# Layer 0 of a graph network: whole-array and half-array products in alternation, one-hots in batches

## The chip, the cores and the metric

The kernel runs on one core of a Trainium2 chip. The metric is device time in microseconds (us) of a whole execution; the median of three runs is compared. Engines are named as the profile names them: PE does matrix products (PEld is its weight load), DVE is the vector engine, ACT the scalar engine, POOL the GpSimd engine, SP the one that issues most DMAs.

## The reference

A graph has 12,500 nodes with 64 features and 212,500 directed edges sorted by destination. Three layers each add up the features of a node's sources, divide by their count and mix with two small matrices; after them, the edges' own attributes are averaged per node and a three-layer perceptron follows.

```python
def _sage_conv(x, src, dst, Wl, Wr, b, n_nodes):
    msgs = x[src]
    summed = jax.ops.segment_sum(msgs, dst, num_segments=n_nodes)
    cnt = jax.ops.segment_sum(jnp.ones(src.shape[0], x.dtype), dst, num_segments=n_nodes)
    agg = summed / jnp.maximum(cnt, 1.0)[:, None]
    return agg @ Wl + x @ Wr + b

h = jnp.maximum(_layernorm(x, axis=-1), 0.0)
x = x + _L0_gnn_ref(h, edge_index, Wl, Wr, b)     # three _sage_conv, relu between
h = jnp.maximum(_layernorm(x, axis=-1), 0.0)
x = x + _L1_gnn_ref(h, edge_index, edge_attr_64, W0, b0, W1, b1, W2, b2)
```

## The kernel before

Nodes are cut into 98 blocks of 128 (`NB`). The sums over edges are done as dense products: the adjacency is written out as a matrix of small counts in 8 bits, two of them in one 16-bit word, and every sum is a product of node rows with a column stripe of that matrix. Layer 0 builds the matrix, uses each stripe from on-chip memory as soon as it is complete, and stores it to DRAM; layers 1 and 2 load the stripes again.

**A stage of layer 0** is one pair of destination blocks (`hp`, 49 of them, a stripe of 256 columns). The rows are held as three bf16 parts of 64 columns each, so that their sum carries the full number. `dense` therefore makes two products per source block: the first two parts together, 128 weight columns, over the whole array into `p1` (L234), and the third part, 64 columns, over half of the array into one half of `p2` (L243). The half alternates with the source block's number, so two neighbouring half products can run at the same time. In the kernel before, all 98 whole products come first, then ACT copies `p1` to `e1` (L239), then come all 98 half products, and DVE adds both into `agg` (L248).

**Building the next stripe** is woven into the stage's 196 products. A list of "fills" has a due time each, as a fraction of the stage; `woven` calls a fill when the products emitted so far reach it. Twenty-six of them are `pair`s: DVE makes for each of two groups of edges a one-hot `c` of 245 columns (L439) and a one-hot with weight `h` of 128 columns (L443), PE multiplies them into `pb` (L447), and ACT writes the counts into the stripe `m` (L450). The 27th stores the stripe through SP's queue. The one-hots have six buffers each, `pb` three, `m` three.

**The other fills.** `turn` (due at 0.05) transposes the stage before's own rows with a half-array product (L260), and `finish` (0.15) mixes `agg` and these rows with the layer's weights (`mix`, L269 and L273, both whole-array) and cuts the result into the three parts for layer 1. `index(j)` (due at 0.6 of every second stage) finds the edges of four destination blocks: one comparison over all tile heads on DVE (L340), three gathers on POOL (L330), counts on DVE, five small products (L397) and a transpose (L406) on PE, and the unpacking of the transposed code into `lo`, `weight` and `col` on DVE (L408 to L426). Its result is used two stages later.

PE's order is the order in which the program is written (`manual_schedule`); a planner orders the other engines' queues. Ahead of the first stage the first two `index` calls, a layer norm over all rows (14 groups, mostly on DVE) and the first stripe are done.

**Layers 1 and 2** call the same `dense` with four destination blocks (512 columns) and loaded stripes.

Of the kernel before, what the change touches and what calls it, by code (L numbers as in the profile page):

```python
# [9 lines left out]
F32 = mybir.dt.float32  # L10
I32 = mybir.dt.int32
BF16 = mybir.dt.bfloat16
# [3 lines left out]
ALU = mybir.AluOpType  # L16
AX = mybir.AxisListType
PSUM = bass.MemoryType.PSUM
# [3 lines left out]
P = 128  # L22
D = 64
# [11 lines left out]
QW, Q5 = 26, 24  # L35
WD = 5
# [24 lines left out]
def in_order(  # L61
# [24 lines left out]
    nc = tc.nc  # L86
    NB, T, EP = sz.nb, sz.t, sz.ep
    NL = Wl.shape[0]
    assert NB % 2 == 0
    HP = NB // 2  # L90
    CW = HP * WD
    NG = -(-NB // 4)
# [104 lines left out]
    ps_d = ctx.enter_context(tc.tile_pool(name="ps_dense", bufs=1, space=PSUM))  # L197
    ps_c = ctx.enter_context(tc.tile_pool(name="ps_conv", bufs=1, space=PSUM))
# [30 lines left out]
    def dense(rows, at, n):  # L229


        p1 = ps_d.tile([P, 4 * P], F32, name="p1")[:, :n]
        for i in range(NB):
            nc.tensor.matmul(  # L234
                p1, rows[:, i, : 2 * D], at(i), start=i == 0, stop=i == NB - 1
            )
            yield
        e1 = conv_p.tile([P, 4 * P], F32, name="e1", bufs=1)[:, :n]
        nc.scalar.copy(e1, p1)  # L239
        p2 = ps_d.tile([P, 4 * P], F32, name="p2")[:, :n]  # L240
        for i in range(NB):
            half = slice(D * (i % 2), D * (i % 2) + D)
            nc.tensor.matmul(  # L243
                p2[half], rows[:, i, 2 * D :], at(i), start=i < 2, stop=i >= NB - 2
            )
            yield
        agg = conv_p.tile([P, 4 * P], F32, name="agg")[:, :n]
        nc.vector.tensor_tensor(agg, e1, p2, op=ALU.add)  # L248
        return agg

    def conv(layer, rows, agg, j0, n):

        ht = hts[conv.turn]
        conv.turn ^= 1

        def turn():
            pt = ps_c.tile([D, 4, P], F32, name="pt")
            for k in range(n):
                for i in range(3):
                    nc.tensor.matmul(  # L260
                        pt[:, k, :], rows[:, j0 + k, D * i : D * i + D], identb,
                        start=i == 0, stop=i == 2,
                    )
            nc.scalar.copy(ht[:D, :n, :], pt[:, :n, :])

        def mix():
            po = ps_c.tile([P, 2, 4, D], F32, name="po")
            for k in range(n):
                nc.tensor.matmul(  # L269
                    po[:, 0, k, :], agg[:, k * P : (k + 1) * P], wl2[:, layer, :],  # L270
                    start=True, stop=True,
                )
                nc.tensor.matmul(  # L273
                    po[:, 1, k, :], ht[:, k, :], wr1[:, layer, :], start=True, stop=True
                )
            o = conv_p.tile([P, 4, D], F32, name="o")[:, :n, :]
            nc.vector.tensor_tensor(  # L277
                o, po[:, 0, :n, :], inv[:, j0 : j0 + n, None].to_broadcast([P, n, D]), op=ALU.mult
            )
            nc.vector.tensor_tensor(o, o, po[:, 1, :n, :], op=ALU.add)  # L280
            return o

        return turn, mix
# [19 lines left out]
    with ExitStack() as s:  # L303
        idx = s.enter_context(tc.tile_pool(name="idx", bufs=2))
        ps_b = s.enter_context(tc.tile_pool(name="ps_build", bufs=3, space=PSUM))
        ps_i = s.enter_context(tc.tile_pool(name="ps_idx", bufs=1, space=PSUM))
        hot = s.enter_context(tc.tile_pool(name="hot", bufs=6))
        ln = s.enter_context(tc.tile_pool(name="ln", bufs=1))
# [16 lines left out]
        mats = s.enter_context(tc.tile_pool(name="mats", bufs=3))  # L325
# [9 lines left out]
        def index(j):  # L335
# [53 lines left out]

# [4 lines left out]
            )  # L394
            pi = ps_i.tile([P, 2, P], F32, name="pi")
# [15 lines left out]
            lo = idx.tile([P, P], F32, name="lo")  # L411
            weight = idx.tile([P, P], F32, name="weight")
            col = idx.tile([P, P], F32, name="col")
            nc.vector.tensor_scalar(a, ci, P - 1, None, op0=ALU.bitwise_and)
            nc.vector.tensor_copy(lo, a)
# [3 lines left out]
            nc.vector.tensor_scalar(weight, b, 255.0, 1.0, op0=ALU.mult, op1=ALU.add)  # L419
# [6 lines left out]
            nc.vector.scalar_tensor_tensor(col, a, float(WD), b, op0=ALU.mult, op1=ALU.add)  # L426
            return lo, weight, col

        def build(m, block, codes):

            lo, weight, col = codes
            off = P * (block % 2)

            def pair(q):
                pb = ps_b.tile([P, 2, 256], F32, name="pb")
                for i in range(2):
                    w = 32 * (block % 4) + q + i
                    c = hot.tile([P, CW], BF16, name="c")
                    nc.vector.tensor_scalar(  # L439
                        c, iota_c, col[:, w : w + 1], None, op0=ALU.is_equal  # L440
                    )
                    h = hot.tile([P, P], BF16, name="h")
                    nc.vector.tensor_scalar(  # L443
                        h, iota_l, lo[:, w : w + 1], weight[:, w : w + 1],
                        op0=ALU.is_equal, op1=ALU.mult,
                    )
                    nc.tensor.matmul(pb[:, i, :CW], h, c, start=True, stop=True)  # L447
                k = WD if q < Q5 else WD - 1
                o = off + WD * q - max(q - Q5, 0)
                nc.scalar.copy(  # L450
                    m[:, :, o : o + 2 * k].rearrange("p h (w d) -> p h w d", d=k),
                    pb[:, :, :CW].rearrange("p w (h d) -> p h w d", d=WD)[:, :, :, :k],
                )

            return [lambda q=q: pair(q) for q in range(0, QW, 2)]

        codes = {}
# [15 lines left out]
        def start_rows(a0):  # L473
            n = min(LG, NB - a0)
            xb = ln.tile([P, n, D], F32, name="xb", bufs=2)
            nc.sync.dma_start(xb, xv[:, a0 : a0 + n, :])
            relu_parts(ln, normed(ln, xb, n), parts[0][:, a0 : a0 + n, :])

        codes[0] = index(0)
        for a0 in range(0, NB, LG):  # L480
            start_rows(a0)
        with tc.manual_schedule(engines={PE}):
            codes[1] = index(1)
            m, fills = matrix(0)
            for f in fills:
                f()
            later = []
            for hp in range(HP):
# [4 lines left out]
                if hp % 2 == 0 and hp // 2 + 2 < NG:  # L493
                    j = hp // 2 + 2
                    fills.append((0.6, lambda j=j: codes.__setitem__(j, index(j))))
                view = m.bitcast(FP8)
                agg = woven(
                    dense(parts[0], lambda i: view[:, i // 2, i % 2 :: 2], 2 * P), fills
                )
                turn, mix = conv(0, parts[0], agg, 2 * hp, 2)  # L500
# [46 lines left out]
    with ExitStack() as s:  # L547
        mats = s.enter_context(tc.tile_pool(name="mats2", bufs=9, reuse_waits="tile"))
# [14 lines left out]
        with tc.manual_schedule(engines={PE}):  # L563
            later = []
            for g in range(NG):
                j0, n = 4 * g, min(4, NB - 4 * g)
                at = columns(g)
                agg = woven(dense(parts[1], at, n * P), later)
                turn, mix = conv(1, parts[1], agg, j0, n)
# [113 lines left out]
            for g in range(NG):  # L683
# [5 lines left out]
                agg = woven(dense(parts[0], at, n * P), fills)  # L689
                turn, mix = conv(2, parts[0], agg, j0, n)  # L690
# [569 lines left out]
```

## Time and profile before

| what | value |
|---|---|
| median of 3 runs | 3512.79 us (3512.18 to 3514.45) |
| the profiled execution | 3514.05 us, of which the span from first to last instruction is 3512.3 us |
| granted PE clock, mean over the span | 0.992 |
| PE busy / DVE busy / ACT busy / POOL busy | 3350.0 / 2111.3 / 1196.0 / 750.7 us |
| first product of layer 0, last L248 of layer 0 | 104.01 us, 1444.33 us |
| first product of layer 1 | 1450.66 us |

Times inside an execution count from its first instruction. A line such as "L243" is a line of the kernel before. In the timeline a row merges neighbouring instructions of one line: start, length, engine, line, operation, tiles, shape, count, and in brackets how long the engine had been idle and what ended that. An instruction's length on PE is modelled and longer than the distance to the next one, so distances between starts are what counts. In a group's row the part after the first bar is the total busy time and the mean length of one in nanoseconds, and after the second the idle time before them.

### The profile page before, as it was taken

What the parts mean: (1) busy time and instruction counts of PE and PEld (TensorE: products, weight loads), DVE (VectorE), ACT (ScalarE), POOL (GpSimd) and SP (SyncE); (2) the same over time, 40 slices, a digit from 0 to 9 for tenths busy, and PEclk for the clock granted to TensorE, in tenths of its full rate; (3) what the DMA queues carried; (4) which work ended last, traced back from release to release, by engine and by line L of the source; (5) the groups of instructions that cost most, each with busy time, mean ns of one, the idle gap of its engine ahead of it and who ended that gap; (6) DMA issues with size and microseconds to landing.
All of it is one profiled execution on the core that took longest, in us unless ns stands there. A gap on an engine that the chain in (4) does not pass through costs nothing.

```text
span 3512.3 us, 69396 instructions
## 1 busy us (share of the span) xinstructions
PE 3350.0 (95%) x26430; PEld 2019.0 (57%) x26430; DVE 2111.3 (60%) x9072; ACT 1196.0 (34%) x2101; POOL 750.7 (21%) x482
## 2 busy tenths in 40 slices
PE   1899999999999999999999999979999999999998
PEld 0566777777777777555454545544555555555555
DVE  8999999999999999300000000035556555555554
ACT  4555555555555555100000000022322322322232
POOL 1000000000000000000000000055555565555562
PEclk9999999999999999999999999989999999999999
DMA  2222222332223223645454545455455555555551
GB/s 45 115 116 118 115 116 115 137 129 115 115 120 146 115 111 134 233 155 220 155 212 165 202 176 191 170 218 181 176 182 211 204 206 181 176 183 211 204 193 53
DMA packets 168554, 555.12 MB, mean 158 GB/s; under 512 B 57793, under 2 KB 60386, under 8 KB 161938
## 3 DMA queue, kind: packets, MB, share of 16 engines
q1 hardware_dynamic: 133232, 478.53, 35.7%
q0 software_dynamic: 19648, 66.90, 5.6%
q10 hardware_dynamic: 15330, 5.16, 0.6%
q8 instruction: 208, 3.41, 0.4%
q14 instruction: 136, 1.11, 0.1%
HBM read 389.97 MB, written 160.56 MB: 157 GB/s over the span
## 4 chain that ended last, share of the span: by engine, by line
PE 84%; DVE 10%; issue 4%; DMA 1%; ACT 1%; POOL 0%; ACTq 0%; SPq 0%; DVEq 0%; POOLq 0%
PE p L234 40%; PE p L243 24%; PE pb L447 8%; PE pe L631 5%; DVE h L443 2%; DVE c L439 2%; PE po L273 2%; PE po L269 2%; PE pt L260 2%; DVE own L627 2%; PE ph L666 1%; PE mo L674 1%; DVE lower L340 0%; DVE junk L385 0%; PE mt L659 0%
## 5 line engine op out<-in xcount | busy, mean ns | idle before, releaser
L234 PEld LDWEIGHTS <-parts 128*128 128x128 bf16 x9702 | 937.2, 99 | 584.7 <-issue 46.2
L234 PE MATMUL p<-t,parts 128*128 128x512 fp8e3 (+1 forms) x4900 | 1106.7, 376 | 4.6 <-DMA t<-mat 4.6
L450 ACT CAST m<-pb 128x490 uint16<-128x490 f32 (+1 forms) x1274 | 717.4, 563 | 537.3 <-PE pb L447 534.4
L627 DVE TENSOR_SCALAR own<-iota_l,eplace 128x128 bf16<-128x128 bf16 x1862 | 548.2, 353 | 401.8 <-PE pe L631 401.4
L443 DVE TENSOR_SCALAR h<-iota_l,lo,weight 128x128 bf16<-128x128 bf16 x2548 | 779.8, 306 | 0.0
L439 DVE TENSOR_SCALAR c<-iota_c,col 128x245 bf16<-128x245 bf16 x2548 | 716.5, 281 | 10.9 <-PE pb L447 5.5
L243 PEld LDWEIGHTS <-parts 128*64 128x64 bf16 x9702 | 494.1, 109 | 387.8 <-issue 185.1
L234 PE MATMUL p<-m,parts 128*128 128x256 fp8e3 x4802 | 652.3, 273 | 0.6 <-ACT m L450 0.6
L243 PE MATMUL p<-t,parts 128*64 128x512 fp8e3 (+1 forms) x4900 | 584.4, 378 | 0.0
L447 PE MATMUL pb<-c,h 128*128 128x245 bf16 x2548 | 499.0, 274 | 52.4 <-DVE h L443 35.0
L248 DVE TENSOR_TENSOR agg<-e,p 128x256 f32<-128x256 f32 (+1 forms) x99 | 54.4, 549 | 603.2 <-PE p L243 600.3
L243 PE MATMUL p<-m,parts 128*64 128x256 fp8e3 x4802 | 409.3, 281 | 0.0
L602 POOL DMA_INDIRECT raw<-in_edge_dram,mine x98 | 93.7, 956 | 1124.9 <-DMA t<-mat 1098.6
L447 PEld LDWEIGHTS <-h 128*128 128x128 bf16 x2548 | 205.6, 98 | 204.0 <-DVE h L443 148.9
L613 POOL TENSOR_TENSOR erest<-raw,cut 128x1216 f32<-128x1216 f32 x98 | 244.2, 2492 | 202.2 <-issue 198.1
L631 PE MATMUL pe<-cut,own 128*128 128x192 bf16 x1862 | 227.0, 248 | 34.9 <-DVE own L627 17.5
L631 PEld LDWEIGHTS <-own 128*128 128x128 bf16 x1862 | 151.3, 98 | 166.4 <-issue 58.6
L615 POOL TENSOR_TENSOR cut<-erest,cut 128x1216 bf16<-128x1216 f32 x98 | 244.6, 2496 | 11.2 <-ACT cut L614 2.6
L612 ACT CAST cut<-raw 128x1216 bf16<-128x1216 f32 x98 | 118.1, 1205 | 275.6 <-PE pe L631 266.0
L277 DVE TENSOR_TENSOR o<-po,inv 128x128 f32<-128x128 f32 (+1 forms) x99 | 35.1, 354 | 271.8 <-PE po L273 271.6
L614 ACT CAST cut<-erest 128x1216 bf16<-128x1216 f32 x98 | 118.1, 1205 | 225.6 <-POOL erest L613 225.6
L330 POOL DMA_INDIRECT to<-in_dst_dram,at_i x25 | 23.6, 946 | 709.6 <-DVE at_i L358 595.8
(143 smaller groups left out, 1666.8 us busy)
## 6 DMA issues: line engine op xcount, KB each, us to landing
t<-mat SPq DMA_DIRECT2D x686, 448.0 KB, 6.1
mat<-m SPq DMA_DIRECT2D x49, 3136.0 KB, 10.0
xb<-in_x_dram SPq DMA_DIRECT2D x14, 224.0 KB, 2.7
xr<-in_x_dram ACTq DMA_DIRECT2D x24, 128.0 KB, 2.2
out_dram<-o SPq DMA_DIRECT2D x24, 128.0 KB, 2.0
raw<-in_edge_dram,mine POOLq DMA_INDIRECT x98, 5.4
eto<-in_dst_dram,mine POOLq DMA_INDIRECT x98, 3.7
here<-in_dst_dram ACTq DMA_DIRECT2D x4, 208.0 KB, 5.5
```

The lines of the kernel that those rows point to most:

```text
L234: nc.tensor.matmul(p1, rows[:, i, : 2 * D], at(i), start=i == 0, stop=i == NB - 1)
L243: nc.tensor.matmul(p2[half], rows[:, i, 2 * D :], at(i), start=i < 2, stop=i >= NB - 2)
L439: nc.vector.tensor_scalar(c, iota_c, col[:, w : w + 1], None, op0=ALU.is_equal)
L443: nc.vector.tensor_scalar(h, iota_l, lo[:, w : w + 1], weight[:, w : w + 1], op0=ALU.is_equal, op1=ALU.mult,)
L447: nc.tensor.matmul(pb[:, i, :CW], h, c, start=True, stop=True)
L450: nc.scalar.copy(m[:, :, o : o + 2 * k].rearrange("p h (w d) -> p h w d", d=k), pb[:, :, :CW].rearrange("p w (h d) -> p h w d", d=WD)[:, : ...
L612: nc.scalar.copy(cut[:, :, :D], raw)
L613: nc.gpsimd.tensor_tensor(rest, raw, cut[:, :, :D], op=ALU.subtract)
L614: nc.scalar.copy(cut[:, :, D : 2 * D], rest)
L615: nc.gpsimd.tensor_tensor(cut[:, :, 2 * D :], rest, cut[:, :, D : 2 * D], op=ALU.subtract)
L627: nc.vector.tensor_scalar(o, iota_l, place[:, k : k + 1], 1.0 / UNIT, op0=ALU.is_equal, op1=ALU.mult,)
L631: nc.tensor.matmul(state["p"], o, cut[:, k, :], start=k == 0, stop=k == EK - 1)
```

## The change

- `dense` takes a step. In layer 0 it is 2: two whole products, then the two half products of the same source blocks, and so on. In layers 1 and 2 the step is all blocks, which is the order before.
- `p1` and `p2` of layer 0 have two buffers. To make room[...], the turn and the mix share one tile and `pb` has two buffers.
- The one-hots of a block's 26 groups are made in three batches of 10, 8 and 8, each by three DVE operations on two tensors: `c`, `h`, and `h` times weight. `lo`, `weight` and `col` are kept in bf16, each number twice in a row, so that a batch can read them as pairs; `c` is one column wider (246). The batches have two buffers.
- `index` ends before its PE work; `by_edge` does that and the unpacking, one stage later.
- The layer norm's buffers are released before the stages start, and `m` has two buffers.

```diff
-    def dense(rows, at, n):
-        p1 = ps_d.tile([P, 4 * P], F32, name="p1")[:, :n]
-        for i in range(NB):
-            nc.tensor.matmul(
-                p1, rows[:, i, : 2 * D], at(i), start=i == 0, stop=i == NB - 1
-            )
-            yield
-        e1 = conv_p.tile([P, 4 * P], F32, name="e1", bufs=1)[:, :n]
-        nc.scalar.copy(e1, p1)
-        p2 = ps_d.tile([P, 4 * P], F32, name="p2")[:, :n]
-        for i in range(NB):
-            half = slice(D * (i % 2), D * (i % 2) + D)
-            nc.tensor.matmul(
-                p2[half], rows[:, i, 2 * D :], at(i), start=i < 2, stop=i >= NB - 2
-            )
-            yield
+    def dense(pool, rows, at, n, step):
+        p1 = pool.tile([P, n], F32, name="p1")
+        p2 = pool.tile([P, n], F32, name="p2")
+        for i0 in range(0, NB, step):
+            blocks = range(i0, min(i0 + step, NB))
+            for i in blocks:
+                nc.tensor.matmul(
+                    p1, rows[:, i, : 2 * D], at(i), start=i == 0, stop=i == NB - 1
+                )
+                yield
+            if i == NB - 1:
+                e1 = conv_p.tile([P, 4 * P], F32, name="e1", bufs=1)[:, :n]
+                nc.scalar.copy(e1, p1)
+            for i in blocks:
+                half = slice(D * (i % 2), D * (i % 2) + D)
+                nc.tensor.matmul(
+                    p2[half], rows[:, i, 2 * D :], at(i), start=i < 2, stop=i >= NB - 2
+                )
+                yield
...
-            pt = ps_c.tile([D, 4, P], F32, name="pt")
+            if layer:
+                pt = pool.tile([D, 4, P], F32, name="pt")
+                space["po"] = pool.tile([P, 2, 4, D], F32, name="po")
+            else:
+                both = pool.tile([P, 2, 2 * P], F32, name="pt_po")
+                pt = both[:D, 0, :].rearrange("p (k n) -> p k n", n=P)
+                space["po"] = both[:, 1, :].rearrange("p (i k d) -> p i k d", i=2, d=D)
...
-        ps_b = s.enter_context(tc.tile_pool(name="ps_build", bufs=3, space=PSUM))
+        ps_d = s.enter_context(tc.tile_pool(name="ps_dense", bufs=2, space=PSUM))
+        ps_c = s.enter_context(tc.tile_pool(name="ps_conv", bufs=1, space=PSUM))
+        ps_b = s.enter_context(tc.tile_pool(name="ps_build", bufs=2, space=PSUM))
         ps_i = s.enter_context(tc.tile_pool(name="ps_idx", bufs=1, space=PSUM))
-        hot = s.enter_context(tc.tile_pool(name="hot", bufs=6))
-        ln = s.enter_context(tc.tile_pool(name="ln", bufs=1))
+        hot = s.enter_context(tc.tile_pool(name="hot", bufs=2))
...
-            lo = idx.tile([P, P], F32, name="lo")
-            weight = idx.tile([P, P], F32, name="weight")
-            col = idx.tile([P, P], F32, name="col")
+            lo = idx.tile([P, P, 2], BF16, name="lo")
+            weight = idx.tile([P, P, 2], BF16, name="weight")
+            col = idx.tile([P, P, 2], BF16, name="col")
+            twice = lambda t: t[:, :, None].to_broadcast([P, P, 2])
...
+            cuts = [(0, 10), (10, 18), (18, QW)]
+            ready = {}
+
+            def hots(q0, q1):
+                n = q1 - q0
+                w = 32 * (block % 4) + q0
+                pairs = lambda t, k: t.rearrange("p (k t) -> p k t", t=2)[:, None].to_broadcast(
+                    [P, n, k // 2, 2]
+                )
+                own = lambda t, k: t[:, w : w + n, None, :].to_broadcast([P, n, k // 2, 2])
+                split = lambda t: t[:, :n].rearrange("p w (k t) -> p w k t", t=2)
+                c = hot.tile([P, 10, CW], BF16, name="c")
+                nc.vector.tensor_tensor(
+                    split(c), pairs(iota_c, CW), own(col, CW), op=ALU.is_equal
+                )
+                h = hot.tile([P, 10, P], BF16, name="h")
+                nc.vector.tensor_tensor(split(h), pairs(iota_l, P), own(lo, P), op=ALU.is_equal)
+                nc.vector.tensor_tensor(split(h), split(h), own(weight, P), op=ALU.mult)
+                for i in range(n):
+                    ready[q0 + i] = (h[:, i, :], c[:, i, : HP * WD])
 
             def pair(q):
+                for cut in cuts:
+                    if q == cut[0]:
+                        hots(*cut)
                 pb = ps_b.tile([P, 2, 256], F32, name="pb")
                 for i in range(2):
-                    w = 32 * (block % 4) + q + i
-                    c = hot.tile([P, CW], BF16, name="c")
-                    nc.vector.tensor_scalar(
-                        c, iota_c, col[:, w : w + 1], None, op0=ALU.is_equal
-                    )
-                    h = hot.tile([P, P], BF16, name="h")
-                    nc.vector.tensor_scalar(
-                        h, iota_l, lo[:, w : w + 1], weight[:, w : w + 1],
-                        op0=ALU.is_equal, op1=ALU.mult,
-                    )
-                    nc.tensor.matmul(pb[:, i, :CW], h, c, start=True, stop=True)
+                    h, c = ready[q + i]
+                    nc.tensor.matmul(pb[:, i, : HP * WD], h, c, start=True, stop=True)
...
-                if hp % 2 == 0 and hp // 2 + 2 < NG:
-                    j = hp // 2 + 2
-                    fills.append((0.6, lambda j=j: codes.__setitem__(j, index(j))))
+                j = hp // 2 + 2
+                if j < NG and hp % 2 == 0:
+                    fills.append((0.6, lambda j=j: found.__setitem__(j, index(j))))
+                elif j < NG:
+                    fills.append((0.6, lambda j=j: codes.__setitem__(j, by_edge(j, *found[j]))))
                 view = m.bitcast(FP8)
                 agg = woven(
-                    dense(parts[0], lambda i: view[:, i // 2, i % 2 :: 2], 2 * P), fills
+                    dense(ps_d, parts[0], lambda i: view[:, i // 2, i % 2 :: 2], 2 * P, 2), fills
                 )
...
-                agg = woven(dense(parts[1], at, n * P), later)
+                agg = woven(dense(ps_d, parts[1], at, n * P, NB), later)
```

## The prediction

> **What bounds the kernel now.** I read the 40 slices first. Layer 0 fills slices 2 to 16; there PE and DVE are both at 9, later PE alone is.
>
> ```profile
> PE   1899999999999999999999999979999999999998
> DVE  8999999999999999300000000035556555555554
> PEclk9999999999999999999999999989999999999999
> ```
>
> PE's busy time is modelled, so it cannot say which of the two sets layer 0. The waits between 104 and 1446 us can: PE waits for DVE 14.3 + 11.5 + 4.3 + 1.7 us and for ACT 0.6 us, 32 us in all. One stage (a pair of destination blocks, 49 of them) ends with L248: from 424.3 to 1213.8 us there are 30 of these, so a stage takes 789.5 / 29 = 27.2 us (27.4 over the whole layer, early stages being slower). **PE sets layer 0**, with DVE close behind.
>
> What PE spends a stage on, its timeline shows (start, length, instructions merged by line, count; L234 whole-array, L243 half-array, L447 one-hot products, L260 the turn, also half-array):
>
> ```profile
> 806.96 0.82 PE L234 MATMUL p<-m,parts 128*128 128x256 fp8e3 x6
> 807.71 0.52 PE L260 MATMUL pt<-identb,parts 128*64 128x128 bf16 x6
> 808.16 0.28 PE L234 MATMUL p<-m,parts 128*128 128x256 fp8e3 x1
> ...
> 819.40 0.93 PE L234 MATMUL p<-m,parts 128*128 128x256 fp8e3 x7
> 820.16 0.37 PE L447 MATMUL pb<-c,h 128*128 128x245 bf16 x2
> 820.37 0.93 PE L234 MATMUL p<-m,parts 128*128 128x256 fp8e3 x7
> 821.14 0.37 PE L447 MATMUL pb<-c,h 128*128 128x245 bf16 x2
> 821.44 0.63 PE L243 MATMUL p<-m,parts 128*64 128x256 fp8e3 x8
> 822.99 0.56 PE L447 MATMUL pb<-c,h 128*128 128x245 bf16 x2 [0.92 <-DVE c L439]
> 823.48 0.62 PE L243 MATMUL p<-m,parts 128*64 128x256 fp8e3 x7
> 824.03 0.38 PE L447 MATMUL pb<-c,h 128*128 128x245 bf16 x2
> 824.35 0.62 PE L243 MATMUL p<-m,parts 128*64 128x256 fp8e3 x7
> 824.90 0.38 PE L447 MATMUL pb<-c,h 128*128 128x245 bf16 x2
> ...
> 1438.68 5.54 PE L243 MATMUL p<-m,parts 128*64 128x256 fp8e3 x98
> 1444.05 0.50 PE L260 MATMUL pt<-identb,parts 128*64 128x128 bf16 x6
> ```
>
> Read starts, not lengths. Seven whole products take 820.16 - 819.40 = 0.76 us, 0.109 each; a pair of L447 among them takes 0.21. Half products run two at a time: 98 take 5.37 us, 0.109 per slot of two. Seven of them (four slots, 0.44) and a pair (0.21) should take 0.65 us, but the period is 824.90 - 824.03 = 0.87. **Leaving half-array mode and coming back costs 0.22 us.** The turn says the same without an L447: six whole products end by 807.61, L260 starts at 807.71; its six at 0.055 end by 808.04, L234 starts at 808.16. Single starts in the trace split it: 0.093 + 0.025 us going in, 0.096 + 0.010 coming out, **0.225 us a round trip**, the smaller terms being the first weight load that nothing hides. None of these instructions waits for another engine.
>
> [...] No row here shows a bf16 two-tensor operation; the change lays its scalars out as adjacent equal pairs[...].
>
> **The change part by part.**
>
> Turns by twos. In the instruction order of the old program layer 0 has 696 runs of half-array work, 14.2 a stage: one per gap between L447 pairs, and the turn. In the new order it has 2689, 54.9 a stage: one for every two blocks, the turn merged into one, and 5.9 where a fill falls between two half products. Outside the first stage that is 47 x 40.7 + 48 (the last stage has no fills) = 1961 more round trips: x 0.225 = **+441 us**, all on PE, which already sets the time. Splitting a slot of two costs 0.109; the new order has 288 splits, the old, by its odd runs, 192: **+10 us**. L447 pairs that now stand next to whole products are counted by this already. If the exposed first loads vanish in runs of two, a trip costs 0.19 and the first term is 373[...].
>
> One-hots batched. Gone: per stage 52 x (L439 + L443); starts 0.415 us apart in DVE's timeline, 21.6 us.
>
> ```profile
> L443 DVE TENSOR_SCALAR h<-iota_l,lo,weight 128x128 bf16<-128x128 bf16 x2548 | 779.8, 306 | 0.0
> L439 DVE TENSOR_SCALAR c<-iota_c,col 128x245 bf16<-128x245 bf16 x2548 | 716.5, 281 | 10.9 <-PE pb L447 5.5
> ```
>
> Added per block: three batches of 10, 8 and 8, 6396 elements of c and twice 3328 of h.[...] DVE's other work is 25.5 - 21.6 = 4 us a stage[...]. What it wins is PE's waits: PE alone needs 26.3 us a stage without index work (L248 at 1347.9 to 1426.7, three stages) and about 0.9 more in every second stage with it (L397 at 851.06 to L243 at 851.85[...]), so 26.7 in the mean; 47 x (27.43 - 26.7) = **-34 us**, the 32 us of the waits view again. Lower bound of the win 0: with only two buffers a batch waits for the batch before last, and behind it on DVE stand the index operations, a stage early for their users, and L248, for which L269 waits only 0.15 of a stage, some 5 us, later.
>
> Index matmuls later. They and their copies only move, by one stage; their three gathers stay on POOL, far from busy, and SP's store isn't passed. The turn of code (L406) waits for DVE's copy of cnt, 0.26 us now[...]. I take 0.[...]
>
> Sums double-buffered: no wait of PE for the copy of p1 or for L248 is in the list, so 0. L447 loses one of three buffers; ACT needs 0.57 us per pair and pairs come every 1.3: 0. The matrix pool loses one of three: its store lands 10 us after its issue, a stage before the buffer is written again: 0.
>
> The start. Until 137.25 us, the first L248, DVE sets the pace (149 of 167 us busy).[...] the first stage's own PE work grows by 9: between -15 and +5, **-7 us**. Layers 1 and 2 keep their order (step = all blocks): 0.
>
> Sum: +441 + 10 - 34 - 7 = **+410 us**. A stage becomes 26.7 + 9.4 = 36.1 us. The profiled execution took 3514.05 us, 1.3 above the median of 3512.79: 3924, so **3923 us**.
>
> **The rivals.**
>
> First loads hidden[...]: 1961 x 0.035 = 69 less, **3855**. For it: only runs of five or more were seen.
>
> DVE comes back:[...] slow reads of a repeated pair.[...] PE waiting up to 2 us a stage, +96: **4020**. For it: no row of this form exists[...].
>
> **Faster: the drain is not paid in a regular alternation**[...]. Then the 696 old trips (157 us) go too: 3514 - 157 - 34 - 7 + 30 for split slots = **3346**. It turns to a gain from a round trip below (34 + 7 - 10) / 1961 = 0.016 us. Against: L234 to L260 and L243 to L234 are the very neighbours the new order has, and each is seen paying, with no wait.
>
> That it doesn't do what it says is no case: the new order has the alternation.
>
> **How the numbers follow.** Full price 0.63, hidden loads 0.15, DVE back 0.14, faster 0.07, something that cancels 0.01. A measurement of this kernel can tell 0.2%, 7 us, from none. The range takes in both slower rivals' inner parts: 3845 to 4000.
>
> **What would show it.** L234, L243 in twos with about 0.55 us per two blocks (0.109 + 0.109 + 0.109 + 0.225), stages of 36 us, last L248 of layer 0 near 1855 us;[...] PE waits for DVE below 34 us. Wrong: whole to half starts 0.11 us apart, or DVE still full.

## The result and the profile after

| | before | after |
|---|---|---|
| median | 3513.46 us (4 runs, 3512.18 to 3514.45) | **3942.32 us** (4 runs, 3939.59 to 3944.91) |
| ratio | | 1.1221, 95% interval 1.1201 to 1.1240 |
| the profiled execution, its span | 3514.05, 3512.3 us | 3944.91, 3943.2 us |
| PE busy, DVE busy | 3350.0, 2111.3 us | 3806.1, 1781.7 us |
| first product, first and last sum (`agg`) of layer 0 | 104.01, 137.25, 1444.33 us | 78.98, 137.84, 1872.52 us |

The change is 12% slower, and nearly all of it lies in layer 0: its last sum comes 428.2 us later, and from there to the end of the span it is 2070.7 us against 2068.0. The lines of the kernel after: L236 is the whole-array product, L245 the half-array one, L250 the sum into `agg`, L462, L466 and L467 the batches of `c` and `h`, L478 the one-hot products, L481 ACT's copy into the stripe, L339 the gathers, L374 the operation that turns gathered words into places.

The 40 slices of the kernel after, the rows of PE, DVE and the granted clock:

```profile
PE   3899999999999999999999999998999999999998
DVE  8756556556556555453000000001555555555554
PEclk9899999999999999999999999998999999999999
```

Layer 0 now reaches into the 19th slice of 98.6 us, where before it reached into the 17th of 87.8. PE is full, and DVE, which stood at 9 beside it, has fallen to about half: the batches did relieve it (its busy time fell by 329.6 us), and the layer is longer. Nothing was made of that relief, since PE had become slower. The clock has no part in it: between the stages' sums its mean was 1.00 of full speed before (138 to 1444 us) as after (181 to 1872 us).

What PE does, in its timeline of the kernel after (start, length, line, count):

```profile
901.45 0.30 PE L245 MATMUL p<-m,parts 128*64 128x256 fp8e3 x2
901.68 0.39 PE L236 MATMUL p<-m,parts 128*128 128x256 fp8e3 x2
902.01 0.30 PE L245 MATMUL p<-m,parts 128*64 128x256 fp8e3 x2
```

Two blocks, four products, take 902.01 - 901.45 = 0.56 us. From the start of two half products to that of two whole ones it is 0.23 us, and from there to the next half products 0.33. No row has a bracket: nothing is waited for. DVE's batches of `c` in the page:

```profile
L462 DVE TENSOR_TENSOR c<-iota_c,col 128x1968 bf16<-128x1968 bf16 (+1 forms) x294 | 373.2, 1269 | 461.8 <-PE pb L478 461.8
```

The wait has turned round: DVE now idles 461.8 us ahead of its batches, until PE lets go of the one-hots; before it was 10.9 us. The waits of PE between 85 and 1875 us (total, times, longest):

```profile
PE pb L478 <- DVE h L467: 14.3, 2, 7.3
PE pi L418 <- DVE cnt L413: 5.9, 23, 0.3
PE pb L478 <- ACT m L481: 4.1, 1, 4.1
```

Some 24 us, and 18 of them are three waits before 152 us, in the start. In the steady part PE waits for nobody but 0.3 us for the counts in every second stage. Its stages last 35.96 and 36.38 us in turn, 36.2 in the mean; between the same sums (the fifth to the 45th) it was 27.4 before.

### The profile page after: what moved, and what is told of

The parts are those of the page before. It is cut to its first block, busy times and chain, and to the rows that moved or that the text cites. A ratio compares the mean times of both kernels' runs of the same rounds, so it can differ in the third digit from the quotient of the medians.

```text
span 3943.2 us, 63742 instructions
## 1 busy us (share of the span) xinstructions
PE 3806.1 (97%) x26430; PEld 1914.6 (49%) x26430; DVE 1781.7 (45%) x4858; ACT 1198.6 (30%) x2101; POOL 755.3 (19%) x482
## 4 chain that ended last, share of the span: by engine, by line
PE 93%; DVE 4%; DMA 1%; issue 1%; ACT 0%; POOL 0%; DVEq 0%; SPq 0%; ACTq 0%; POOLq 0%
PE p L236 45%; PE p L245 28%; PE pb L478 8%; PE pe L667 4%; DVE own L663 2%; PE ph L702 1%; PE po L282 1%; PE po L278 1%; PE pt L269 1%; PE mo L710 1%; PE pt_po L282 1%; PE pt_po L269 1%; PE pt_po L278 0%; PE mt L695 0%; DMA of<-in_src_dram,at_i 0%
## 5 line engine op out<-in xcount | busy, mean ns | idle before, releaser
L236 PEld LDWEIGHTS <-parts 128*128 128x128 bf16 x9702 | 794.0, 98 | 783.2 <-issue 46.5
L236 PE MATMUL p<-t,parts 128*128 128x512 fp8e3 (+1 forms) x4900 | 1106.9, 376 | 4.7 <-DMA t<-mat 4.7
L481 ACT CAST m<-pb 128x490 uint16<-128x490 f32 (+1 forms) x1274 | 716.2, 563 | 918.0 <-PE pb L478 913.6
L236 PE MATMUL p<-m,parts 128*128 128x256 fp8e3 x4802 | 989.1, 278 | 0.0
L245 PEld LDWEIGHTS <-parts 128*64 128x64 bf16 x9702 | 552.1, 108 | 807.9 <-issue 606.1
L245 PE MATMUL p<-m,parts 128*64 128x256 fp8e3 x4802 | 808.2, 298 | 0.0
L663 DVE TENSOR_SCALAR own<-iota_l,eplace 128x128 bf16<-128x128 bf16 x1862 | 515.7, 337 | 436.2 <-PE pe L667 422.2
L245 PE MATMUL p<-t,parts 128*64 128x512 fp8e3 (+1 forms) x4900 | 584.4, 378 | 0.0
L462 DVE TENSOR_TENSOR c<-iota_c,col 128x1968 bf16<-128x1968 bf16 (+1 forms) x294 | 373.2, 1269 | 461.8 <-PE pb L478 461.8
L478 PE MATMUL pb<-c,h 128*128 128x245 bf16 x2548 | 491.4, 276 | 49.5 <-DVE h L467 42.0
L250 DVE TENSOR_TENSOR agg<-e,p 128x256 f32<-128x256 f32 (+1 forms) x99 | 54.3, 549 | 596.5 <-PE p L245 572.7
L339 POOL DMA_INDIRECT to<-in_dst_dram,at_i x25 | 26.7, 1066 | 1299.7 <-DVE at_i L367 1299.0
L478 PEld LDWEIGHTS <-h 128*128 128x128 bf16 x2548 | 200.0, 98 | 145.4 <-DVE h L467 45.7
L467 DVE TENSOR_TENSOR h<-h,weight 128x1024 bf16<-128x1024 bf16 (+1 forms) x294 | 215.7, 734 | 5.0
L466 DVE TENSOR_TENSOR h<-iota_l,lo 128x1024 bf16<-128x1024 bf16 (+1 forms) x294 | 214.5, 730 | 0.0
```

The source lines that it names most:

```text
L236: nc.tensor.matmul(p1, rows[:, i, : 2 * D], at(i), start=i == 0, stop=i == NB - 1)
L245: nc.tensor.matmul(p2[half], rows[:, i, 2 * D :], at(i), start=i < 2, stop=i >= NB - 2)
L462: nc.vector.tensor_tensor(split(c), pairs(iota_c, CW), own(col, CW), op=ALU.is_equal)
L466: nc.vector.tensor_tensor(split(h), pairs(iota_l, P), own(lo, P), op=ALU.is_equal)
L467: nc.vector.tensor_tensor(split(h), split(h), own(weight, P), op=ALU.mult)
L478: nc.tensor.matmul(pb[:, i, : HP * WD], h, c, start=True, stop=True)
```

## The experiments

The theory to be tested: each passage from half-array to whole-array work and back costs 0.225 us of PE, and the number of passages alone makes the loss. The rivals: the batches or their buffers slow the stage, or the change of one stage for the index work does. "Trips" below are runs of half-array work in a stage, counted in the traces' order between two sums.

**One part alone, and the other alone.** `e2_turns_only` is the kernel before with the alternation (`dense` takes a step, as in the change) and nothing else of the change:

```diff
...
-                    dense(parts[0], lambda i: view[:, i // 2, i % 2 :: 2], 2 * P), fills
+                    dense(parts[0], lambda i: view[:, i // 2, i % 2 :: 2], 2 * P, 2), fills
```

> The kernel before with the products of layer 0 in turns by twos and nothing else (sums single-buffered, one-hots single, index as before). Theory: 54.9 round trips a stage, stages of 36.0 to 36.6 us plus up to 1 us in which PE waits for the single sums' readers, 3985 us (3950 to 4010), as slow as the whole change or slower. Rival (the loss comes from the other parts): within 50 us of the kernel before, 3513 us.

Measured 3967.66 us, ratio 1.1301 (1.1282 to 1.1320): 455 us above the kernel before, as expected, where the prediction's terms for trips and splits make 451. That the two lie so close is in part chance: from first to last sum it takes 442.9 us longer, PE's waits there having fallen from 28.5 to 20.8 us, and its first sum comes 8.7 us later. The alternation alone is the loss, batches or no batches.

`e1_products_apart` is the kernel after with the order of products taken back, everything else kept:

```diff
-                    dense(ps_d, parts[0], lambda i: view[:, i // 2, i % 2 :: 2], 2 * P, 2), fills
+                    dense(ps_d, parts[0], lambda i: view[:, i // 2, i % 2 :: 2], 2 * P, NB), fills
```

> The changed kernel with the step of layer 0 back to all blocks; batches, double sums and the later index matmuls stay. Theory (each passage from the whole array to half of it and back costs 0.225 us, and nothing else in the change costs time): 14.2 round trips a stage again, stages of 26.3 and 27.2 us in turn, PE's waits for DVE in layer 0 mostly gone, 3475 us (3460 to 3495), below the kernel before. Rival (the batches, the shared buffers or the index matmuls cost a good part of the 430 us): clearly above the kernel before, over 3600 us.

Measured 3569.34 us, ratio 1.0161 (1.0144 to 1.0178). Without the alternation the loss shrinks to some 13% of its size, but the rest of the change, expected to gain 37 us, loses 57; the time lies between the theory's range and the rival's. Something in it costs what the long stages of the kernel after conceal; it is taken up below.

**The number of trips as a dial.** `e3_step6` takes turns by six blocks, `e5_whole_third` keeps the turns by two but makes the third part's products over the whole array, so that no mode changes remain among the products:

```diff
-                    dense(ps_d, parts[0], lambda i: view[:, i // 2, i % 2 :: 2], 2 * P, 2), fills
+                    dense(ps_d, parts[0], lambda i: view[:, i // 2, i % 2 :: 2], 2 * P, 6), fills
```

> The changed kernel with a step of 6 in place of 2: six whole products, six half products, in turn. The written order has 28.2 round trips a stage (14.2 with all blocks, 54.9 with twos). Theory (cost in proportion to the round trips): about 29.7 and 30.5 us a stage, 3640 us (3620 to 3665). Rival (the cost belongs to short runs as such, a run of two that never gets its weights in time, not to the passage): near 3480 us, since runs of six are as long as those of the kernel before.

Measured 3642.03 us, ratio 1.0369 (1.0351 to 1.0386): 28.5 trips and stages of 30.2 us, as expected of a cost that goes with the number of trips; from here to stages of 36.2 us with 55.0 trips it is some 0.23 us a trip, so runs of six pay about what runs of two do.

```diff
+                if step == 2:
+                    nc.tensor.matmul(
+                        p2, rows[:, i, D:], at(i), start=i == 0, stop=i == NB - 1
+                    )
+                    yield
+                    continue
```

> The changed kernel, still in turns by twos, but in layer 0 the third part's product takes 128 weight columns (second and third part together) over the whole array, so that the array's mode never changes between the two kinds; the second part is then summed twice, and the layer's numbers are not the reference's. PE streams twice as many columns for p2: 98 x 0.109 in place of 49 x 0.109 us. Theory: 1 round trip a stage (the turn), stages of 28.0 to 28.7 us, 3570 us (3550 to 3590), 370 us faster than the change although PE does more. Rival (alternating between two sums, or between two memories of results, is what costs, whatever the mode): slower than the change, over 3942 us, as PE does more.

Measured 3577.45 us, ratio 1.0182 (1.0165 to 1.0199). Of its 28.7 us a stage, 98 third products at 0.109 are 10.7, where half products two at a time need 5.3. It does twice the array's work for them and is still 365 us faster than the kernel after, since one trip a stage is left, the turn. This too is as expected. So it is the change of mode that costs, not the turns themselves.

**Where the 57 us come from.** In the trace of `e1_products_apart` the stages are 27.2 us and some 30.5 us in turn, and the long ones are those with the gathers. Its waits from 75 to 1510 us, without the three engines' mere waiting for work:

```profile
DVE place L374 <- DMA to<-in_dst_dram,at_i: 85.5, 21, 5.4
ACT parts L218 <- DVE o L289: 78.2, 21, 5.2
PE pb L478 <- ACT m L481: 54.1, 31, 3.8
```

The timelines of DVE, ACT and PE in one such stage tell how the first becomes the last:

```profile
752.82 0.28 DVE L374 TENSOR_SCALAR place<-to,node 128x128 f32<-128x128 int32 x1 [3.60 <-DMA to<-in_dst_dram,at_i]
753.02 0.28 DVE L289 TENSOR_TENSOR o<-o,pt_po 128x128 f32<-128x128 f32 x1
...
753.34 0.31 ACT L218 ACTIVATE parts<-o 128x128 bf16<-128x128 f32 x1 [3.12 <-DVE o L289]
753.55 0.55 ACT L481 CAST m<-pb 128x490 uint16<-128x490 f32 x1
...
754.15 0.37 PE L478 MATMUL pb<-c,h 128*128 128x245 bf16 x2 [1.96 <-ACT m L481]
```

DVE stands at L374 for a gathered list. The second operation of the mix (L289) is behind it; ACT waits at L218 for that, with its copy L481 behind; PE has filled both `pb` buffers and waits for the copy. Why is the list late? The part of the DMA view by issue, first the kernel before from 656 to 664 us, then `e1_products_apart` from 689 to 697 us; the last number is the time from issue to landing:

```profile
to<-in_dst_dram,at_i POOLq DMA_INDIRECT x1, 2.5
```

```profile
q1 hardware_dynamic: 128, 2.81, 87.2%
...
to<-in_dst_dram,at_i POOLq DMA_INDIRECT x1, 5.7
```

In the kernel before the gather ran alone. In the other it was issued at 691.1 us, 3.7 us after the stripe's store (at 687.4), and beside it q1 took 87% of the 16 DMA engines. The gather took 5.7 us from issue to landing there, and 2.5 alone. In the kernel after the gather comes 2.3 us ahead of the store (684.1 and 686.4 us), and L374, 4.3 us after the gather's issue, doesn't wait. The second half of the cause is the planner: in the kernel before it left 16 us between the gather (766.1) and its reader (782.4); in `e1_products_apart` DVE comes to the reader 2.4 us after the gather (746.8) and stands there for 3.6 us. That the store makes the list late is read from these traces; no run moves the store alone.

A first attempt to take the wait away only recorded the gathers a stage earlier (`e8_apart_gather_early`, `e1_products_apart` with `index` split into the gathers and `places`):

```diff
-                    fills.append((0.6, lambda j=j: found.__setitem__(j, index(j))))
+                    fills.append((0.6, lambda j=j: away.__setitem__(j, index(j))))
...
+                    fills.append((0.6, lambda j=j: found.__setitem__(j, places(j, *away[j]))))
```

> The changed kernel with the step back to all blocks (as in the first experiment, 3569 us) and index cut in two: its gathers are issued one stage ahead of the operations that read them. Theory (with the products apart, DVE stands in its queue at L374 for a gather still on its way, behind it the mix's addition, behind that ACT's copies and so PE's next one-hot product; longer stages hide this): every second stage falls from 30.5 to about 27 us, 3490 us (3470 to 3510). Rival (the two buffers of pb or of the batches are the wait): stays above 3540 us.

Measured 3574.74 us, ratio 1.0174 (1.0157 to 1.0191): no gain, for a plain reason. The planner put the reader right behind the gather again, and there it stood until the list had landed, 6.5 us after its issue (668.3 after 661.8 us). The time lies where the rival had it, but the wait that was to go was still there, so it tells nothing of either.

`e10_apart_tied` gives the reader an operand that does not exist before the next stage, so that no order can put it early, and has it due early in that stage:

```diff
+                late = idx.tile([P, 1], F32, name="late")
+                nc.vector.scalar_tensor_tensor(
+                    late, behind_of[:, :1], 0.0, n0, op0=ALU.mult, op1=ALU.add
+                )
+                n0 = late[:, :1]
...
+                    fills.append((0.05, lambda j=j, a=agg: found.__setitem__(j, places(j, *away[j], a))))
```

> As e8_apart_gather_early (all products of the left half of the aggregation in one run, those of the right half in another, everything else as in the changed kernel), with the operation that turns the gathered words into places taking one operand from the sum of the stage before, so that it cannot be put right behind the gather again. If the 57 us by which e1_products_apart stands above the kernel before are VectorE's 85 us of waiting for gathers and what is held behind it, the time falls to 3490 us (3470 to 3515) and no wait of VectorE for the gathered words is left. Rival: the index work in the second stage would hold up TensorE even without that wait; then the wait goes and the time stays above 3540 us.

Measured **3484.61 us**, ratio 0.9918 (0.9902 to 0.9935). The waits of DVE for the gathered list are gone from the list. In DVE's and POOL's timelines the reader, now L385, stands at 701.13 us, 50 us after the gather that it reads:

```profile
651.31 0.94 POOL L339 DMA_INDIRECT to<-in_dst_dram,at_i  x1 [46.65 <-DVE at_i L367]
...
701.13 0.28 DVE L385 TENSOR_SCALAR place<-to,late 128x128 f32<-128x128 int32 x1
```

Stages are 26.3 and 27.4 us. So the 57 us were this wait, with what was held behind it, and the change without the alternation and without the wait is 29 us faster than the kernel before.

PE's clock is among what was held behind it. In the windows view the third number from the right is the mean granted clock, 1.00 being full speed. These are `e1_products_apart` and then `e10_apart_tied`, each from its first to its last sum, and last a stretch of `e1_products_apart` just after the stage shown above:

```profile
139.00:1501.00 1362.00, 1303.63 (x12657) 951.54 (x12656) 949.77 (x1970) 736.13 (x1414) 54.66 (x58) 0.98 0.29 118
136.00:1415.00 1279.00, 1272.31 (x12659) 937.11 (x12657) 969.89 (x2067) 736.44 (x1414) 79.55 (x64) 1.00 0.31 126
...
755.10:758.40 3.30, 3.24 (x17) 2.13 (x16) 3.30 (x15) 1.78 (x4) 0.00 (x0) 0.50 0.02 5
```

PE had stood for 1.96 us until 754.15, and soon after ran 3.3 us at half the clock. Of the 20 waits of PE of 1.68 us or more between these sums, 18 have such a stretch begin within 2 us of their end. Of the 83 us between the two kernels' layers, 52.4 us are PE's waits for ACT's copy in that window, and an estimated 27 us the clock (2% of 1362 us).

`e11_twos_tied` puts the alternation back on top of that (step 2 instead of `NB`, nothing else):

> The changed kernel, turns by twos as they are, with e10_apart_tied's edit: the operation that turns the gathered words into places is tied to the sum of the stage before. The changed kernel's second stage lasts 43.2 us, the later ones 36.2, and in it VectorE waits 6.4 us for a gathered list. If this is the same gather wait that costs e1_products_apart 57 us, the second stage falls to 36 to 37 us and the whole to 3935 us (3930 to 3939), and nothing else moves. Rival: the second stage is long because PE's clock is down and the first matrices are late; then it stays near 43 us and the time at 3942 us.

Measured 3935.68 us, ratio 1.1203 (1.1188 to 1.1218). The second stage is 37.2 us, nearly as expected; that "nothing else moves" was wrong, as the first sum came 5.0 us earlier too (132.8 us). In the steady stages the wait had cost the kernel after nothing.

**The price of a trip.** Kernels in which no gather is waited for in the steady part give it cleanly. Between `e10_apart_tied` and `e11_twos_tied` only the step differs; the other two differ in more and show the trend. Stages between the fifth and the 45th sum:

| kernel | trips a stage | us a stage |
|---|---|---|
| `e9_whole_tied` (below) | 1.0 | 23.91 |
| `e10_apart_tied` | 14.5 | 26.87 |
| `e3_step6` | 28.5 | 30.16 |
| `e11_twos_tied` | 55.0 | 36.18 |

From `e10_apart_tied` to `e11_twos_tied`: 9.31 us, less 0.2 for two more split slots, over 40.5 trips = **0.225 us a trip**.

**The other way: fewer trips than before.** If 14.5 trips cost 3 us a stage, a faster kernel puts all fills among the whole products. `e4_fills_in_whole` does so on the kernel after with step `NB`, `e6_old_fills_in_whole` on the kernel before:

```diff
-                    fills += [((i + 0.5) / len(more), f) for i, f in enumerate(more)]
+                    fills += [((i + 0.5) / len(more) * 0.5, f) for i, f in enumerate(more)]
...
-                later = [(0.05, turn), (0.15, finish)]
+                later = [(0.0, turn), (0.1, finish)]
```

with `index` and `by_edge` due at 0.3.

> The changed kernel with all whole products first and all half products after them, and every fill due in the whole-array part: the one-hot pairs in its first to last product, the turn just ahead of it, the index matmuls at its middle. One round trip a stage is left. Theory (a round trip costs 0.225 us wherever it stands): PE alone 22.8 and 23.5 us a stage; with the gather's wait seen in the first experiment still there, up to 4 us in every second stage: 3390 us (3320 to 3430), below the kernel before. Rival (DVE or ACT can't deliver 26 pairs in 17 us, so that the wait moves there): 3500 us or more.

> The kernel before, with its fills moved in the same way and nothing else. PE alone again 22.8 and 23.5 us a stage, but DVE needs 21.6 us for the one-hots of a stage, 0.415 us each, and can run only three pairs ahead through the half-array part. Theory (DVE now sets the stage): about 27.5 us a stage, no gain, 3515 us (3480 to 3560). Rival (DVE keeps up; the batches were not needed): 3350 us.

Measured 3508.85 us, ratio 0.9985 (0.9978 to 0.9992), and 3705.63 us, ratio 1.0545 (1.0528 to 1.0563). Both are slower than their ranges, each for its own reason. In the old form 52 one-hots of each kind must be made in half a stage: from 104 to 1640 us PE waited 115.9 us for `h`. In the batched form a stage takes 27.2 us in the mean, not the 23 worked out: DVE waited 106.4 us for gathered lists, and PE 83.7 us for the sums that DVE made behind them (L278 for L250). In both the clock fell with the waits: from first to last sum its mean was 0.94 in the old form and 0.96 in the batched one, against 1.00 in the kernel before. What the batches are good for shows only in `e9_whole_tied` below, whose stages take 23.9 us: the old form needs 21.6 us of DVE for the one-hots and some 4 us for the rest (the prediction's figures), more than such a stage lasts. No run puts the old one-hots there.

`e7_best` added more buffers (`pb` four, batches three, `p1` and `p2` one) and the split of `e8_apart_gather_early`:

> Both together, and the buffers set for it: fills in the whole-array part, gathers a stage ahead, the sums single-buffered again[...], so that pb has four buffers, and three buffers of batches. Theory: PE alone sets the stage, 22.8 and 23.5 us, 3310 us (3290 to 3360), faster than the kernel before by 5 to 6 per cent. Rival (ACT's 0.62 us per pair against PE's 0.62 in the whole part, with ACT's other copies on top): 1 to 2 us more a stage, 3370 to 3410 us.

Measured 3453.37 us, ratio 0.9824 (0.9808 to 0.9841), outside its range, with 30.1 us for the second stages and the gather waited for in nearly each (15 times between 300 and 1100 us, up to 4.5 us). `e9_whole_tied` adds the tie, lets the index steps fall due a little later, and makes the first batch of a pair of blocks a stage earlier:

```diff
-            ready = {}
+            ready = ahead.pop(block, {})
...
+                    fills.append((0.12, lambda j=j: found.__setitem__(j, places(j, *away[j], mixed[0][:, 0, :]))))
...
+                    fills.append((0.5, lambda b=b: ahead.__setitem__(b, build(None, b, codes[b // 4]))))
```

> As e7_best, with three more edits in layer 0: the subtraction and comparison that turn the gathered words into places take one operand from the mix's output of the same stage, so that VectorE can come to them only a stage and more after the gather was issued; the index steps fall due a little later; the first batch of one-hots of the next pair of blocks is built in the stage before. e7_best's second stages last 30.1 us against 21.8 us for the others, and VectorE waits 4.5 us for the gather in each. If that wait, and what is held behind it (ScalarE's conversion, the one-hot products), is what the long stages are made of, they fall to some 25 us and the whole to 3340 us (3310 to 3400). Rival: the long stages are long because VectorE's and ScalarE's work for the index no longer fits beside 22 us of products; then the wait is replaced by waits for one-hots, and the time stays at 3420 to 3455 us.

Measured 3352.64 us, ratio 0.9541 (0.9525 to 0.9557), inside its range. What each of the three edits is worth was not measured apart. A stage of it, on PE (every fill is behind it when the half products begin):

```profile
725.55 0.71 PE L236 MATMUL p<-m,parts 128*128 128x256 fp8e3 x5
726.19 5.54 PE L245 MATMUL p<-m,parts 128*64 128x256 fp8e3 x98
731.56 0.50 PE L269 MATMUL pt_po<-identb,parts 128*64 128x128 bf16 x6
```

The largest of PE's waits that are left, from 75 to 1270 us, is for the counts:

```profile
PE pi L429 <- DVE cnt L424: 23.0, 24, 1.1
```

`e12_counts_early` puts the counting products 0.05 of a stage ahead of that:

> e9_whole_tied, with the five index products that count (L420) made a fill of their own, due 0.05 of a stage before the transpose that follows them. In e9_whole_tied TensorE waits for VectorE's copy of those counts 23 times, up to 1.1 us each, 25 us in all, because the transpose goes into the same buffer. If the wait is only that copy standing behind a batch, it goes, and the time falls by some 23 us to 3330 us (3322 to 3342). Rival: VectorE is as late with the next thing, and TensorE waits there; then 3345 to 3353 us.

Measured **3342.72 us**, ratio 0.9516 (0.9503 to 0.9529), the fastest here, but just above what was expected: the wait shrank only from 23.0 to 16.9 us. The copy stands not so much behind a batch, as was thought, as behind the next index call's comparison over all tile heads, which takes DVE 1.94 us:

```profile
741.73 1.94 DVE L349 TENSOR_SCALAR_CACHE_REDUCE lower<-heads,node 128x1664 bf16<-128x1664 f32 x1
```

The counting products run at 741.11 us, DVE's copy of the counts only at 743.59, and PE, ready earlier, goes on at 743.81. In `e9_whole_tied` the same comparison stands ahead of 20 of the 25 copies.

## Why the prediction was right

It gave 3923 us in 3845 to 4000, slower with a chance of 0.92 (0.63, 0.15 and 0.14); the median is 3942.32. The 428 us of layer 0 against its +410:

- **The trip, 0.225 us: right.** The table above gives 0.225, and one sees it in every two blocks: 0.56 us where 0.55 was forecast. What the exposed first loads cost did not vanish in runs of two, so that rival is out. So is the faster rival, by the same table: a trip of the regular alternation took the same 0.225 us as one of the kernel before. (The "drain" of that rival is the author's name for what the distance between two starts gains at a passage, 0.093 us going in and 0.096 coming out; what the array does in that time no trace shows.) That it is the change between the two kinds of products that is paid for is what `e5_whole_third` shows: without it a stage took 28.7 us instead of 36.2.
- **Trips and splits, +441 +10, PE's waits, -34: right in size, but the waits were put to the wrong account.** From first to last sum the kernel after takes 427.6 us longer, where these terms make 417. Of the 10.6 us, 7.0 are the one long second stage (43.2 against 36.2), the remaining 3.6 are under 0.1 us a stage. The waits' term was credited to the batches. But `e2_turns_only` has no batches, and PE waits for no one-hot in its layer 0 either: stages of 36 us hide them already. On PE the batches pay only without the alternation, where `e10_apart_tied` takes 27.6 us less than the kernel before from first to last sum.
- **The batches, DVE no longer full: right.** DVE's timeline of the kernel after, with 10 groups:

```profile
880.41 1.44 DVE L462 TENSOR_TENSOR c<-iota_c,col 128x2460 bf16<-128x2460 bf16 x1 [2.26 <-PE pb L478]
881.77 0.82 DVE L466 TENSOR_TENSOR h<-iota_l,lo 128x1280 bf16<-128x1280 bf16 x1
882.62 0.83 DVE L467 TENSOR_TENSOR h<-h,weight 128x1280 bf16<-128x1280 bf16 x1
```

  From `c` to `h` it is 1.36 us for 2460 elements; with 8 groups it is 1.10 us for 1968 (885.48 to 886.58 us). So the 492 elements between them take 0.26 us, 0.53 ns each. The three operations for 10 groups take 3.0 us, where ten pairs of single one-hots took 4.15 (0.415 each). How much DVE would need in the new form was the author's estimate: the trace before has no such operation. With DVE at half load, "DVE comes back" is out.
- **Index products one stage later, 0: right.** PE waits 0.3 us for the counts, 23 times, 5.9 us in all; before it was 11.5 us. It was right for this load only: in `e9_whole_tied`, with denser stages, the same wait is 1.0 us in the mean.
- **Sums, `pb` and stripe buffers, 0: right for the kernel after.** No such wait is in the list beyond one of 4.1 us in the start. But beside the alternation the second buffers of the sums are worth something; in `e2_turns_only`, which has one of each, the first whole product of a stage waits for ACT's copy:

```profile
PE p L237 <- ACT e L243: 13.4, 47, 0.3
```

  In `e1_products_apart`, where stages are shorter, the two `pb` buffers pass a delay of ACT on to PE.
- **The start, -7: wrong**, by 14.6 us in all. The first sum came 0.6 us later instead of 7 earlier, and the next stage took 7.0 us more than a steady one. The working counted DVE's saved time, an estimate of the author's that no trace had shown, and PE's added one, but no wait for a gather. DVE waits for one in the kernel after as well, in the second stage:

```profile
145.25 0.28 DVE L374 TENSOR_SCALAR place<-to,node 128x128 f32<-128x128 int32 x1 [6.39 <-DMA to<-in_dst_dram,at_i]
```

  Behind it PE waited 4.1 us for ACT's copy at 151.57 us. `e11_twos_tied`, which has no such wait, gets 6.0 of the second stage's 7.0 us back. The first stage is another matter: there PE waited twice, until 86.96 and 122.64 us, for `h` behind DVE's layer norm and index work, and in `e11_twos_tied`, where DVE's order differs, only once (with 3.5 us for the layer norm's parts); its first sum comes 5.0 us earlier. The second idle time cost more than itself. These are the windows of the kernel after around it, and below them its second stage:

```profile
115.00:122.60 7.60, 0.37 (x3) 0.11 (x1) 7.60 (x21) 2.59 (x5) 0.00 (x0) 0.82 0.00 1
122.60:130.00 7.40, 7.37 (x33) 2.74 (x33) 5.79 (x13) 3.32 (x7) 0.95 (x1) 0.50 0.01 3
130.00:138.00 8.00, 8.00 (x59) 3.63 (x58) 7.88 (x16) 3.83 (x8) 2.87 (x3) 0.99 0.34 109
...
138.00:181.00 43.00, 38.61 (x259) 17.92 (x258) 28.52 (x95) 14.99 (x29) 6.26 (x7) 0.88 0.21 82
```

  After 7.3 us of idling PE ran for 7.4 us at a granted clock of 0.50, then at 0.99. In the second stage the mean clock was 0.88; that of `e11_twos_tied`, without the wait, was 1.00 (138 to 175 us). In the kernel after it was 0.50 from 151.6 to 159 us, behind the wait of 4.1 us; in `e1_products_apart` it was 0.50 for 3.3 us soon after a wait of 1.96 us. How the first stage's 7.6 us divide between DVE's order and the clock is not settled by a run.

One sentence of the working was wrong without harm to the number: that the gathers "stay on POOL, far from busy, and SP's store isn't passed". POOL's load was not the question. What mattered, as these traces have it, is when the list lands beside the store, and how soon DVE's order comes to its reader. In the long stages of the kernel after this costs nothing; without the alternation it is worth 57 - (-29) = 86 us. That is also why the parts don't add up: alternation alone +455, all else alone +57, together +429. With the wait gone they nearly do: +455 and -29 make +426, and `e11_twos_tied` stands at +422.5.

## What to carry to other kernels

Count the changes between whole-array and half-array products in the order of the program, price one from a place where the trace already shows it, and multiply; here the two kinds were cheapest in two long runs, with all other work among the whole-array ones (23.91 us a stage with 1.0 trip, 36.18 with 55.0). Before calling a reordered step free, look for what was hidden behind the slack that it had: the gather issued 3.7 us after the large store landed late here (5.7 us after its issue, 2.5 without the store), and the planner put its reader right behind it. Look at the granted clock as well: the 1.96 us for which PE stood in `e1_products_apart` were soon followed by 3.3 us at 0.50. A reader that must not come early is best tied to a value that doesn't exist before then.

## What the runs showed of the hardware

- A trip to half-array products and back cost 0.225 us even as a regular alternation of two and two products, none of which waits; doubling the third part's array work to stay with whole-array products (`e5_whole_third`) was 365 us cheaper.
- The same indirect gather took 2.5 us from issue to landing with the DMA engines free, and 5.7 us (`e1_products_apart`) and 6.5 us (`e8_apart_gather_early`) beside the store of 3136 KB.
- After 7.3 us without work PE's granted clock was 0.50 for 7.4 us, and after 1.96 us (`e1_products_apart`) for 3.3 us. In `e9_whole_tied`, where PE's waits from 140 to 1250 us are 1.1 us at most, its mean was 1.00.
